# Four graph layers on one core: the first layer's sparse product in two float32r parts, its mask widened by GpSimd

## The chip, the core and the metric

The kernel runs on one core of a Trainium2 chip. The metric is the device time of one execution in microseconds; the median of three is compared. The engines are named as in the profile: PE is TensorE (PEld its weight loads), DVE VectorE, ACT ScalarE, POOL GpSimd, SP SyncE, which here issues most DMAs.

## The reference

Inputs are x (2708 rows of 128), adj (2708 x 2708, some 8 ones per row, each row divided by its count, so that it is a 0/1 mask times one value per row), and small weights. Four layers, each applied to a layer norm with relu and added to x:

```python
h = relu(layernorm(x));  x = x + L0(h, adj)     # hyperbolic: see below
h = relu(layernorm(x));  x = x + L1(h, adj)     # messages gelu(s_i + d_j + b), summed over edges, then an update
h = relu(layernorm(x));  x = x + relu(adj @ (h @ W2))
h = relu(layernorm(x));  x = x + h @ W_self + (adj @ h / deg) @ W_neigh

# L0, in short
h     = exp0(log0(x) @ embed);  h = h_add(h, embed_bias)
neigh = exp0(adj @ log0(h))                      # the sparse product of this case
out   = h_add(exp0(log0(concat(x, neigh)) @ layer), layer_bias)
```

exp0 and log0 scale a row by tanh(n)/n and arctanh(n)/n of its norm n.

## The kernel before

Rows are cut into T = 22 tiles of 128 (the last has 20 rows). Columns of the products go in blocks of four tiles, 512 columns, so there are 6 blocks; the last has 148 columns. `adj_t` is read in pieces of four row tiles by one block (`read_piece`), and each piece is turned into an fp8 0/1 `mask` by VectorE or ScalarE.

The sparse product of layer 0 is `yT = u^T mask`: for each block and each tile t, TensorE multiplies a 128x128 weight made of u's rows by `mask[:, t, block]` and adds into one PSUM bank. To keep float32 precision with an fp8 mask, `split` writes u as three bf16 parts that add up to it, and `add_product` issues one matmul for each part. `end_product` squares the sums into `hT`'s space and copies them to yT, from which `neighbours` takes norms, the product with `layer_w` and the row `own`. `update` then brings x forward for a list of blocks, normalises it, turns it with TensorE (`normal_tiles` into hT), multiplies by `msg_w` and writes d to two tables in HBM, `d_early` (first three blocks) and `d_hbm` (all).

Beside the product runs the search for the edges. `pack` sums the mask times powers of two, so that one word holds 22 tiles (the same mask columns as the product), `find_words` takes the 24 largest words of a row, `find_columns` and `lay_out` turn them into indices, and `pack_edges` into lists of edges. GpSimd's indirect DMAs then gather rows of d: 44 early ones (`gather_early`, from d_early), and in layer 1's loop 152 more (`messages`).

The code calls blocks in a hand-written order: product 0, 1 in two halves with the search for block 2 between, 2, neighbours of the first three, 3, three quarters of 4, update of the first three, first early gathers, the rest of 4, 5, then the search's remainder, pack_edges of the first three, neighbours and update of the last three. This is program order; a scheduler places the instructions within each engine's queue. After it, from layer 1's loop on, a planner with durations and due times writes the order, and `manual_schedule` keeps it.

SBUF space is handed out from pools on two sides. On the right side lie, before, `hT` (pool turned) and the low bf16 parts (pool parted); the same bf16 parts are used again in layers 1 and 2. The third layer widens its mask to float32r (`widen`, ScalarE) and uses two parts already.

Of the kernel before, what the change touches and what calls it, by code (L numbers as in the profile page):

```python
# [29 lines left out]
F32 = mybir.dt.float32  # L30
# [529 lines left out]
def sparse_stack(  # L560
# [37 lines left out]
    def cols(t0, t1):  # L598
        return slice(t0 * P, min(t1 * P, N))
# [12 lines left out]
    hT_held = ExitStack()  # L612
    hT = hT_held.enter_context(tc.tile_pool(name="turned", bufs=1, side="right")).tile(
        [P, NP], F32, name="hT"
    )
    tmp = upper.tile([P, T, D], F32, name="tmp")
    parted = min(16, T)
    parts_held = ExitStack()
    parts_low = parts_held.enter_context(tc.tile_pool(name="parted", bufs=1, side="right")).tile(
        [P, parted, 3, D], BF16, name="parts"  # L620
    )
    parts_high = state.tile([P, max(1, T - parted), 3, D], BF16, name="partsh")
# [123 lines left out]
    d_early = dram.tile([first_half * P + 1, D], F32, name="d_early")  # L746
    none = const.tile([1, D], F32, name="none")
    nc.gpsimd.memset(none, BIG)
    msg_w, msg_br, upd_w, upd_br, ln_wr, ln_br, w2_w, self_w, neigh_w = (
# [13 lines left out]

    def load_later():

        nc.gpsimd.dma_start(out=d_hbm[NP : NP + 1, :], in_=none)
        nc.gpsimd.dma_start(out=d_early[first_half * P :, :], in_=none)
        for w, src in (
            (msg_w, msg_wt),
            (upd_w, upd_wt),  # L770
            (w2_w, w2),
            (self_w, w_self),
            (neigh_w, w_neigh),
        ):
            nc.gpsimd.dma_start(out=w, in_=src.rearrange("(a p) o -> p a o", p=P))
        for r, src in ((msg_br, msg_b), (upd_br, upd_b), (ln_wr, ln_w), (ln_br, ln_b)):
            nc.gpsimd.dma_start(out=r, in_=src.partition_broadcast(P))
# [18 lines left out]

    def split(src, sl, left):

        nc.scalar.copy(part_of(sl, 0), src[:, sl, :])  # L799
        nc.vector.tensor_sub(left, src[:, sl, :], part_of(sl, 0))  # L800
        nc.scalar.copy(part_of(sl, 1), left)
        nc.vector.tensor_sub(part_of(sl, 2), left, part_of(sl, 1))  # L802


    unchecked = list(range(T))
# [5 lines left out]
    with ExitStack() as st:  # L811

        words_p = st.enter_context(tc.tile_pool(name="words", bufs=2))
        left_p = st.enter_context(tc.tile_pool(name="left", bufs=2))
        wide = st.enter_context(tc.tile_pool(name="wide0", bufs=1))
        small = st.enter_context(tc.tile_pool(name="small", bufs=1))
        pair_p = st.enter_context(tc.tile_pool(name="pair", bufs=2))
        ps_acc = st.enter_context(tc.tile_pool(name="ps_acc", bufs=2, space=PSUM))
# [7 lines left out]
        for t in range(T):  # L826
            nc.gpsimd.tensor_scalar_mul(shifts[:, t, :], ident, float(2 ** (T - 1 - t)))
# [4 lines left out]
        load_later()  # L832

# [135 lines left out]
        cand = spare[:, n_top : 4 * n_top].rearrange("p (t k s) -> p t k s", k=3, s=SLOTS)  # L969
        more = wide.tile([P, T], F32, name="more")  # L970

        def read_piece(b, g, vector=False, after=None):
# [231 lines left out]
        def pack_edges(b, after=None):  # L1204
# [5 lines left out]
            for k in range(n):  # L1210
                t = t0 + k
                before = pair_p.tile([P, EDGES], F16, tag="before", name=f"before{t}")
                with queue_behind(after):
# [12 lines left out]
                for q in range(NQ):  # L1226
# [6 lines left out]
                    )  # L1233
            ex = small.tile([P, BLOCK, NQ, TAIL + 3], F32, tag="ex", name=f"exs{b}")
            nc.scalar.copy(ex[:, :n], px[:, :, :, : TAIL + 3])
            m = n * NQ
            kth, past, jump = (
                small.tile([P, BLOCK * NQ], F32, tag=name, name=f"{name}{b}")[:, :m]
                for name in ("kth", "past", "jump")
            )  # L1240
            flat_ex = ex.rearrange("p t q c -> p (t q) c")[:, :m, :]
            edge = small.tile([P, BLOCK, NQ], F32, tag="edge", name=f"edge{b}")[:, :n, :]
            nc.vector.tensor_copy(edge, edge_p.unsqueeze(1).to_broadcast([P, n, NQ]))
# [11 lines left out]
            nc.vector.tensor_add(kth, kth, jump)  # L1255
            sel = small.tile([P, BLOCK * NQ, TAIL], F32, tag="sel", name=f"sel{b}")[:, :m, :]
            nc.vector.tensor_tensor(
# [5 lines left out]
            nc.vector.tensor_mul(sel, sel, flat_ex[:, :, :TAIL])  # L1263
            cf = small.tile([P, BLOCK * NQ], F32, tag="cf", name=f"cf{b}")[:, :m]
            nc.vector.tensor_reduce(cf, sel, AX.X, ALU.add)
# [7 lines left out]

        def begin_product(b):
            return ps_acc.tile([P, BANK], F32, tag="acc", name=f"acc{b}")

        def add_product(b, acc, ts, after=None):

            sl = cols(*blocks[b])
            w = sl.stop - sl.start  # L1280
            for t in ts:
                for k in range(3):
                    with queue_behind(after):
                        last = nc.tensor.matmul(  # L1284
                            acc[:, :w],
                            part_of(t, k),
                            mask[:, t, sl],
                            start=(t == 0 and k == 0),
                            stop=(t == T - 1 and k == 2),
                        )  # L1290
            return last

        def end_product(b, acc, sums):
# [4 lines left out]
            w = sl.stop - sl.start  # L1298
            sq = hT[:, t0 * P : t1 * P]
            if w < n * P:  # L1300
                nc.gpsimd.memset(sq[:, w : n * P], 0.0)
            nc.scalar.activation(sq[:, :w], acc[:, :w], AF.Square)
            nc.scalar.copy(yT[:, sl], acc[:, :w])
            ps, first = sums
            for k in range(n):
# [3 lines left out]
                )  # L1309

        def product(b, sums):
            acc = begin_product(b)
            add_product(b, acc, range(T))
            end_product(b, acc, sums)

        def neighbours(bs, sums):
# [21 lines left out]
            for b in bs:  # L1338
                g = groups[b]
                ps = tiles_times(g, yT, layer_w[:, 1, :], f"ne{b}")  # L1340
                for t in range(g.start, g.stop):
# [8 lines left out]
                    nc.scalar.activation(  # L1350
                        hT[:, t * P : (t + 1) * P],
                        own[:, t, :],
# [103 lines left out]
        nc.vector.tensor_mul(ca, ca, f)  # L1456
        scaled = nc.vector.tensor_mul(cb, cb, f)
        for g in pieces[:3] if nb > 1 else ():
            read_piece(1, g)
        for g, sl in enumerate(groups):  # L1460
            for t in range(sl.start, sl.stop):
# [12 lines left out]
        for g, sl in enumerate(groups):  # L1474
            nc.scalar.copy(own[:, sl, :], tiles_times(sl, hT, layer_w[:, 0, :], f"own{g}"))
        if NP > N:
# [20 lines left out]
        find_columns(groups[0])  # L1497
        product(0, sums)
        find_words(1, words_in(1), scaled)
        find_columns(groups[1])  # L1500
        acc = begin_product(1)
        add_product(1, acc, range(T // 2))
        find_words(2, words_in(2), scaled)
        find_columns(groups[2])
        read_block(3)
        add_product(1, acc, range(T // 2, T))
        end_product(1, acc, sums)
        lay_out(halves[0])
        find_words(3, words_in(3))
        read_block(4)  # L1510
        product(2, sums)
        neighbours([0, 1, 2], sums)
        read_block(5)
        sums = sums_of(late)
        product(3, sums)
# [24 lines left out]
        for b in late:  # L1540
            pack_edges(b)


# [1130 lines left out]
```

## Time and profile before

| | |
|---|---|
| measured runs | 549.23 us median (548.35 to 553.0) |
| profiled execution, its own time | 653.21 us |
| its span | 651.4 us |
| PE, DVE, ACT, POOL busy | 430.5, 412.4, 321.0, 224.0 us |
| granted TensorE clock, mean | 0.825 |
| DMA | 77.85 MB, mean 120 GB/s |

The profile is of one execution, which took longer than the measured runs. Busy time is summed over an engine's instructions; for TensorE the ends are modelled. A line like `L1284 PE MATMUL acc<-mask,parts` names the source line, the engine, the operation, and the output and inputs by tile. Line numbers in the prediction are those of the kernel before. The chain of waits goes back from the last instruction, at each step to what released it. "another core or an unknown queue" there means that no instruction in the trace accounts for the release.

### The profile page before, as it was taken

The numbers are of one execution on the slowest core, as the hardware profiler recorded it, in microseconds if no ns is written. First come the engines' busy times: TensorE is split into PE (matmuls) and PEld (weight loads), VectorE is DVE, ScalarE is ACT, GpSimd is POOL, SyncE is SP. The second block draws the span as 40 slices with busy tenths as digits, with TensorE's granted clock in tenths as the row PEclk, the third lists the DMA queues.
The fourth block names the chain that finished last, engine by engine and source line by source line (L and its number), as shares of the span: only waits on it lengthen the run. The fifth ranks groups of instructions, "written<-read, shape, count | busy, mean of one in ns | idle before, by whom it ended". The sixth has DMA issues, their size and how long they took to land.

```text
span 651.4 us, 8164 instructions
## 1 busy us (share of the span) xinstructions
PE 430.5 (66%) x2467; PEld 295.6 (45%) x2467; DVE 412.4 (63%) x1715; ACT 321.0 (49%) x634; POOL 224.0 (34%) x277
## 2 busy tenths in 40 slices
PE   2956999999930003632177777837577888899875
PEld 2642444756720002532064544534445544678764
DVE  6879596578832166642155654565567648799963
ACT  3788677714200122321043533746567662899821
POOL 8500000000477700277465655665676300000000
PEclk9987999799955555666558987967799889999979
DMA  8884798200321100121131112665475240017502
GB/s 282 265 288 151 260 351 284 79 2 10 110 52 50 48 1 12 37 52 52 34 88 41 41 41 78 225 204 192 148 254 167 94 165 7 2 37 291 198 18 74
DMA packets 39363, 77.85 MB, mean 120 GB/s; under 512 B 5231, under 2 KB 18151, under 8 KB 38267
## 3 DMA queue, kind: packets, MB, share of 16 engines
q1 hardware_dynamic: 30846, 63.15, 28.3%
q0 software_dynamic: 6720, 13.38, 8.0%
q10 hardware_dynamic: 1744, 0.72, 0.4%
q8 instruction: 21, 0.34, 0.2%
q14 instruction: 32, 0.25, 0.1%
HBM read 73.62 MB, written 3.62 MB: 119 GB/s over the span
## 4 chain that ended last, share of the span: by engine, by line
PE 37%; DVE 25%; another core or an unknown queue 14%; ACT 13%; issue 5%; DMA 3%; POOL 2%; ACTq 0%; DVEq 0%
PE acc L1284 10%; PE two L2113 7%; DVE eq L2486 4%; ACT eq L2154 3%; PE pk L1021 2%; PE msg L1876 2%; PE three L2300 2%; ACT wm L1709 2%; PE msg L1870 2%; DMA layer_w<-in_L_gnn_layer_dram 2%; PE d L941 1%; POOL g L1810 1%; PE u L1424 1%; PE nd L1333 1%
## 5 line engine op out<-in xcount | busy, mean ns | idle before, releaser
L1810 POOL DMA_INDIRECT g<-d_hbm,head_c x88 | 90.5, 1028 | 106.1 <-DVE v L1751 45.7
L2113 PE MATMUL two<-mask,parts 128*128 128x512 fp8e4 (+1 forms) x288 | 71.1, 385 | 12.7 <-ACT parts L2044 5.7
L1810 POOL DMA_INDIRECT gt<-d_hbm,tail_c x64 | 64.5, 1008 | 24.1 <-issue 18.7
L1487 POOL DMA_INDIRECT early<-d_early,early_c x44 | 44.6, 1013 | 73.1 <-DMA d_hbm<-v 60.0
L2300 PE MATMUL three<-wm,pair 128*128 128x512 f32 (+1 forms) x264 | 62.9, 388 | 1.9 <-ACT pair L2359 1.8
L1284 PE MATMUL acc<-mask,parts 128*128 128x512 fp8e4 (+1 forms) x288 | 59.6, 358 | 0.6 <-DVE parts L802 0.4
L1709 ACT CAST wm<-mask 128x2708 fp32r<-128x2708 fp8e4 x22 | 53.3, 2450 | 7.1 <-DVE u L2064 7.0
L2300 PEld LDWEIGHTS three<-wm,pair 128*128 128x128 f32 x264 | 47.4, 194 | 11.7 <-ACT pair L2359 2.3
L2113 PEld LDWEIGHTS <-parts 128*128 128x128 bf16 x288 | 29.0, 106 | 40.1 <-issue 13.2
L930 PE MATMUL hTpm<-ident,h 128*128 128x128 f32 x22 | 5.1, 350 | 61.0 <-ACT h L920 61.0
L1876 PE MATMUL msg<-rt,gt 128*128 128x128 f32 x128 | 22.4, 318 | 33.5 <-ACT gt L1925 32.3
L1284 PEld LDWEIGHTS <-parts 128*128 128x128 bf16 x288 | 26.7, 99 | 37.8 <-ACT parts L799 7.5
L992 ACT ACTIVATE mask<-a 128x2048 fp8e4<-128x2048 uint32 (+3 forms) x27 | 37.9, 1433 | 9.0 <-DMA a<-in_adj_t_dram 9.0
L1021 PE MATMUL pk<-mask,shifts 128*128 128x512 fp8e4 (+1 forms) x132 | 31.6, 377 | 12.0 <-ACT mask L992 12.0
L1876 PEld LDWEIGHTS msg<-rt,gt 128*128 128x128 f32 x128 | 19.1, 219 | 39.4 <-ACT gt L1925 36.5
L2154 ACT ACTIVATE eq<-eq 128x1354 fp8e4<-128x1354 fp8e4 x26 | 34.4, 1326 | 4.9 <-DVE eq L2148 3.2
L1870 PE MATMUL msg<-ident,g 128*128 128x128 f32 (+1 forms) x176 | 28.3, 311 | 11.8 <-ACT g L1918 9.9
L1886 PE MATMUL msg<-upd_w,aggs 128*128 128x128 f32 x44 | 13.3, 394 | 30.6 <-issue 15.9
L1870 PEld LDWEIGHTS msg<-ident,g 128*128 128x128 f32 (+1 forms) x176 | 25.4, 219 | 16.5 <-ACT g L1918 12.4
L1859 DVE TENSOR_TENSOR gt<-gt,msg 128x384 f32<-128x384 f32 (+1 forms) x22 | 11.9, 540 | 31.4 <-remote 18.6
L930 PEld LDWEIGHTS hTpm<-ident,h 128*128 128x128 f32 x22 | 3.5, 173 | 62.1 <-ACT h L920 61.9
L2486 DVE TENSOR_SCALAR_CACHE_REDUCE eq<-row,val 128x1354 fp8e4<-128x1354 f32 (+1 forms) x18 | 29.2, 1620 | 0.3
(457 smaller groups left out, 1024.7 us busy)
## 6 DMA issues: line engine op xcount, KB each, us to landing
a<-in_adj_t_dram SPq DMA_DIRECT2D x25, 1024.0 KB
hT<-in_adj_dram SPq DMA_DIRECT2D x26, 677.0 KB
row<-in_adj_dram SPq DMA_DIRECT2D x8, 1354.0 KB
a<-in_adj_t_dram SPq DMA_DIRECT2D x5, 296.0 KB
g<-d_hbm,head_c POOLq DMA_INDIRECT x88
a<-in_adj_t_dram SPq DMA_DIRECT2D x5, 256.0 KB
d_hbm<-v SPq DMA_DIRECT2D x5, 256.0 KB
out_dram<-x SPq DMA_DIRECT2D x5, 256.0 KB
```

The source lines that it names most:

```text
L992: nc.scalar.activation(mask[:, g : g + n, sl], bits[:, :n, :w], AF.Sign, saturate=False)
L1021: nc.tensor.matmul(pk[:, :w], shifts[:, t, :], mask[:, t, sl], start=(t == 0), stop=(t == T - 1))
L1284: last = nc.tensor.matmul(acc[:, :w], part_of(t, k), mask[:, t, sl], start=(t == 0 and k == 0), stop=(t == T - 1 and k == 2),)
L1487: nc.gpsimd.indirect_dma_start(out=early_d[t // EACH][:n, t % EACH, k, :], out_offset=None, in_=d_early, in_offset=bass.IndirectOffsetOnAx ...
L1709: nc.scalar.copy(m, mask[:, t, :])
L1810: nc.gpsimd.indirect_dma_start(out=g[:n, q, :], out_offset=None, in_=d_hbm, in_offset=bass.IndirectOffsetOnAxis(ap=table[:n, q : q + 1], a ...
L1870: nc.tensor.matmul(sums(), box["g"][:n, q, :], ident[:n, :], start=False, stop=False)
L1876: nc.tensor.matmul(sums(), box["gt"][:, q, :], box["rt"][:, q, :], start=False, stop=(q == nq - 1),)
L2113: nc.tensor.matmul(two[b][:, : sl.stop - sl.start], part_of(t, k), mask[:, t, sl], start=(t == 0 and k == 0), stop=(t == T - 1 and k == 2),)
L2154: nc.scalar.activation(eq[0][:n, : c1 - c0], eq[0][:n, : c1 - c0], AF.Copy, accum_out=same[:n, t, k : k + 1], saturate=False,)
L2300: nc.tensor.matmul(three[b][:, : sl.stop - sl.start], made["pair"][:, t, k, :], wide_mask[t][:, sl], start=(t == 0 and k == 0), stop=(t == ...
L2486: nc.vector.tensor_scalar(eq[:n, : c1 - c0], my["row"][:n, c0:c1], val[:n, t : t + 1], None, op0=ALU.is_equal, op1=ALU.add, accum_out=same ...
```

## The change

Layer 0's product uses two float32r parts of u: u itself as float32r, and the rest. They lie in six tiles, one per group (pool fresh). [...]the mask has to be widened: GpSimd copies it, piece by piece, into a ring of three buffers (pool pieces), two tiles by 512 columns, or one tile by the 660 columns of blocks 4 and 5 together. Those two blocks are multiplied in one pass, each weight serving both. `product` is a generator that yields after half of the tiles, where block 1 has the search for block 2 between.

To make room, the right side is used in two phases. First `hT` (pool rising), closed once `own` is computed, which now comes before the split; then fresh and pieces; and after the last product these are closed and `hT` (turned), the bf16 parts (parted) and a pool `edges` with the temporaries of `pack_edges` are laid over them. A tile of a new pool waits for the tiles whose space it takes. So `update` of the first three blocks and `pack_edges` come after the last product in the program. The squares go to the space of `tmp` (`sq_room`, `junk`). The row `none` (moved from the constants) and the turned weights `wT` now share the tag and the single buffer of `row_square`.

```diff
-    def split(src, sl, left):
-        nc.scalar.copy(part_of(sl, 0), src[:, sl, :])
-        nc.vector.tensor_sub(left, src[:, sl, :], part_of(sl, 0))
-        nc.scalar.copy(part_of(sl, 1), left)
-        nc.vector.tensor_sub(part_of(sl, 2), left, part_of(sl, 1))
...
+        none = small.tile([1, D], F32, tag="rsq", name="none")
+        nc.gpsimd.memset(none, BIG)
...
-            wT = pair_p.tile([P, P], F32, tag="wT", name=f"wT{name}")
+            wT = small.tile([P, P], F32, tag="rsq", name=f"wT{name}")
...
-                before = pair_p.tile([P, EDGES], F16, tag="before", name=f"before{t}")
+                before = edge_pool().tile([P, EDGES], F16, tag="before", name=f"before{t}", bufs=2)
...
-            for t in ts:
-                for k in range(3):
-                    with queue_behind(after):
-                        last = nc.tensor.matmul(
-                            acc[:, :w], part_of(t, k), mask[:, t, sl],
-                            start=(t == 0 and k == 0), stop=(t == T - 1 and k == 2),
-                        )
...
+        def pieces_of(bs):
+            sl = cols(blocks[bs[0]][0], blocks[bs[-1]][1])
+            n = 2 if len(bs) == 1 else 1
+            w = sl.stop - sl.start
+            for t in range(0, T, n):
+                m = later["ring"].tile([P, 2 * BANK], F32R, tag="piece", name=f"wide{bs[0]}_{t}")
+                m = m[:, : n * w].rearrange("p (n c) -> p n c", n=n)
+                nc.gpsimd.tensor_copy(m, mask[:, t : t + n, sl])
+                for k in range(n):
+                    yield t + k, m[:, k, :]
+
+        def product(bs, sums, some=None):
+            accs = some or [
+                ps_acc.tile([P, BANK], F32, tag="acc", name=f"acc{b}") for b in bs
+            ]
+            for t, m in pieces_of(bs):
+                for k in range(2):
+                    at = 0
+                    for b, acc in zip(bs, accs):
+                        sl = cols(*blocks[b])
+                        w = sl.stop - sl.start
+                        nc.tensor.matmul(
+                            acc[:, :w], two_of(t)[:, k, :], m[:, at : at + w],
+                            start=(t == 0 and k == 0), stop=(t == T - 1 and k == 1),
+                        )
+                        at += w
+                if t == T // 2 - 1:
+                    yield
+            for b, acc in zip(bs, accs):
+                end_product(b, acc, sums)
...
+        for g, sl in enumerate(groups):
+            nc.scalar.copy(own[:, sl, :], tiles_times(sl, hT, layer_w[:, 0, :], f"own{g}"))
+        hT_held.close()
...
-            left = left_p.tile([P, BLOCK, D], F32, tag="left", name=f"left{g}")
-            split(u, sl, left[:, : sl.stop - sl.start, :])
+            two = parts_of[g]
+            nc.scalar.copy(two[:, :, 0, :], u[:, sl, :])
+            nc.vector.tensor_sub(two[:, :, 1, :], u[:, sl, :], two[:, :, 0, :].bitcast(F32))
...
-        acc = begin_product(4)
-        split_at = 3 * T // 4
-        last = add_product(4, acc, range(split_at))
-        formed = update([0, 1, 2], nc.scalar.copy, last)
+        for _ in product([4, 5], sums):
+            pass
+        rising.close()
+        hT = hT_held.enter_context(
+            tc.tile_pool(name="turned", bufs=1, side="right", reuse_waits="tile")
+        ).tile([P, NP], F32, name="hT")
...
+        edges_held = ExitStack()
+        later["edges"] = edges_held.enter_context(
+            tc.tile_pool(name="edges", bufs=1, side="right", reuse_waits="tile")
+        )
+        formed = update([0, 1, 2], nc.scalar.copy, None)
         find_words(4, words[4], formed)
...
-        add_product(4, acc, range(split_at, T), latest["times"])
-        end_product(4, acc, sums)
         find_words(5, words[5], formed)
-        product(5, sums)
```

More of the change, by code (lines that the diff above doesn't have):

```diff
@@ L612, in sparse_stack @@
     hT_held = ExitStack()
-    hT = hT_held.enter_context(tc.tile_pool(name="turned", bufs=1, side="right")).tile(
-        [P, NP], F32, name="hT"
+    hT = hT_held.enter_context(tc.tile_pool(name="rising", bufs=1, side="right")).tile(
+        [P, NP], F32, name="hTr"
     )
@@ L618, in sparse_stack @@
     parts_held = ExitStack()
-    parts_low = parts_held.enter_context(tc.tile_pool(name="parted", bufs=1, side="right")).tile(
-        [P, parted, 3, D], BF16, name="parts"
-    )
     parts_high = state.tile([P, max(1, T - parted), 3, D], BF16, name="partsh")
@@ L746, in sparse_stack @@
     d_early = dram.tile([first_half * P + 1, D], F32, name="d_early")
-    none = const.tile([1, D], F32, name="none")
-    nc.gpsimd.memset(none, BIG)
     msg_w, msg_br, upd_w, upd_br, ln_wr, ln_br, w2_w, self_w, neigh_w = (
@@ L762, in sparse_stack, with load_later @@
     )
-    def load_later():
+    def load_later(none):
         nc.gpsimd.dma_start(out=d_hbm[NP : NP + 1, :], in_=none)
@@ L813, in sparse_stack @@
         words_p = st.enter_context(tc.tile_pool(name="words", bufs=2))
-        left_p = st.enter_context(tc.tile_pool(name="left", bufs=2))
         wide = st.enter_context(tc.tile_pool(name="wide0", bufs=1))
         small = st.enter_context(tc.tile_pool(name="small", bufs=1))
-        pair_p = st.enter_context(tc.tile_pool(name="pair", bufs=2))
         ps_acc = st.enter_context(tc.tile_pool(name="ps_acc", bufs=2, space=PSUM))
@@ L831, in sparse_stack @@
             nc.gpsimd.memset(share_of[:, k : k + 1], 1.0 / max(k, 1))
-        load_later()
+        load_later(none)
         names = {}
@@ L970, in sparse_stack @@
         more = wide.tile([P, T], F32, name="more")
+        sq_room = spare[:, 4 * n_top : 4 * n_top + BANK]
+        junk = spare[:, 4 * n_top + BANK : 4 * n_top + BANK + D]
         def read_piece(b, g, vector=False, after=None):
@@ L1233, in pack_edges @@
                     )
-            ex = small.tile([P, BLOCK, NQ, TAIL + 3], F32, tag="ex", name=f"exs{b}")
+            ex = edge_pool().tile([P, BLOCK, NQ, TAIL + 3], F32, tag="ex", name=f"exs{b}")
             nc.scalar.copy(ex[:, :n], px[:, :, :, : TAIL + 3])
@@ L1237, in pack_edges @@
             kth, past, jump = (
-                small.tile([P, BLOCK * NQ], F32, tag=name, name=f"{name}{b}")[:, :m]
+                edge_pool().tile([P, BLOCK * NQ], F32, tag=name, name=f"{name}{b}")[:, :m]
                 for name in ("kth", "past", "jump")
@@ L1241, in pack_edges @@
             flat_ex = ex.rearrange("p t q c -> p (t q) c")[:, :m, :]
-            edge = small.tile([P, BLOCK, NQ], F32, tag="edge", name=f"edge{b}")[:, :n, :]
+            edge = edge_pool().tile([P, BLOCK, NQ], F32, tag="edge", name=f"edge{b}")[:, :n, :]
             nc.vector.tensor_copy(edge, edge_p.unsqueeze(1).to_broadcast([P, n, NQ]))
@@ L1255, in pack_edges @@
             nc.vector.tensor_add(kth, kth, jump)
-            sel = small.tile([P, BLOCK * NQ, TAIL], F32, tag="sel", name=f"sel{b}")[:, :m, :]
+            sel = edge_pool().tile([P, BLOCK * NQ, TAIL], F32, tag="sel", name=f"sel{b}")[:, :m, :]
             nc.vector.tensor_tensor(
@@ L1263, in pack_edges @@
             nc.vector.tensor_mul(sel, sel, flat_ex[:, :, :TAIL])
-            cf = small.tile([P, BLOCK * NQ], F32, tag="cf", name=f"cf{b}")[:, :m]
+            cf = edge_pool().tile([P, BLOCK * NQ], F32, tag="cf", name=f"cf{b}")[:, :m]
             nc.vector.tensor_reduce(cf, sel, AX.X, ALU.add)
@@ L1272, in sums_of, with edge_pool @@
             return ps_one.tile([P, BANK], F32, tag="one", name=f"nsq{bs[0]}"), blocks[bs[0]][0]
[L1274 to L1279, printed above, removed]
-            w = sl.stop - sl.start
-            for t in ts:
-                for k in range(3):
-                    with queue_behind(after):
-                        last = nc.tensor.matmul(
+        later = {}
+        def edge_pool():
+            return later["edges"]
+        def pieces_of(bs):
+            sl = cols(blocks[bs[0]][0], blocks[bs[-1]][1])
+            n = 2 if len(bs) == 1 else 1
+            w = sl.stop - sl.start
+            for t in range(0, T, n):
[15 more added lines that the diff above has]
+                        nc.tensor.matmul(
                             acc[:, :w],
-                            part_of(t, k),
-                            mask[:, t, sl],
+                            two_of(t)[:, k, :],
+                            m[:, at : at + w],
                             start=(t == 0 and k == 0),
-                            stop=(t == T - 1 and k == 2),
+                            stop=(t == T - 1 and k == 1),
                         )
-            return last
+                        at += w
[3 more added lines that the diff above has]
+                end_product(b, acc, sums)
         def end_product(b, acc, sums):
@@ L1298, in end_product @@
             w = sl.stop - sl.start
-            sq = hT[:, t0 * P : t1 * P]
+            sq = sq_room[:, : n * P]
             if w < n * P:
-                nc.gpsimd.memset(sq[:, w : n * P], 0.0)
+                nc.gpsimd.memset(sq[:, w:], 0.0)
             nc.scalar.activation(sq[:, :w], acc[:, :w], AF.Square)
@@ L1309, in end_product @@
                 )
[L1311 to L1314, printed above, removed]
         def neighbours(bs, sums):
@@ L1350, in neighbours @@
                     nc.scalar.activation(
-                        hT[:, t * P : (t + 1) * P],
+                        junk,
                         own[:, t, :],
@@ L1457, in sparse_stack, with two_of @@
         scaled = nc.vector.tensor_mul(cb, cb, f)
+        for g, sl in enumerate(groups):
+            nc.scalar.copy(own[:, sl, :], tiles_times(sl, hT, layer_w[:, 0, :], f"own{g}"))
+        hT_held.close()
+        rising = ExitStack()
+        fresh = rising.enter_context(
+            tc.tile_pool(name="fresh", bufs=1, side="right", reuse_waits="tile")
+        )
+        parts_of = [
+            fresh.tile([P, sl.stop - sl.start, 2, D], F32R, name=f"fresh{g}")
+            for g, sl in enumerate(groups)
+        ]
+        later["ring"] = rising.enter_context(
+            tc.tile_pool(name="pieces", bufs=3, side="right", reuse_waits="tile")
+        )
+        def two_of(t):
+            return parts_of[t // BLOCK][:, t % BLOCK]
         for g in pieces[:3] if nb > 1 else ():
@@ L1473, in sparse_stack @@
             read_piece(2, g, k < 3, last if k < 3 else None)
-        for g, sl in enumerate(groups):
-            nc.scalar.copy(own[:, sl, :], tiles_times(sl, hT, layer_w[:, 0, :], f"own{g}"))
         if NP > N:
@@ L1497, in sparse_stack @@
         find_columns(groups[0])
-        product(0, sums)
+        for _ in product([0], sums):
+            pass
         find_words(1, words_in(1), scaled)
         find_columns(groups[1])
[L1501 to L1507, printed above, removed]
+        for _ in product([1], sums):
+            find_words(2, words_in(2), scaled)
+            find_columns(groups[2])
+            read_block(3)
         lay_out(halves[0])
@@ L1510, in sparse_stack @@
         read_block(4)
-        product(2, sums)
+        for _ in product([2], sums):
+            pass
         neighbours([0, 1, 2], sums)
@@ L1514, in sparse_stack @@
         sums = sums_of(late)
-        product(3, sums)
+        for _ in product([3], sums):
+            pass
         words = {b: words_in(b) for b in (4, 5)}
-        acc = begin_product(4)
-        split_at = 3 * T // 4
-        last = add_product(4, acc, range(split_at))
-        formed = update([0, 1, 2], nc.scalar.copy, last)
+        for _ in product([4, 5], sums):
+            pass
+        rising.close()
+        hT = hT_held.enter_context(
+            tc.tile_pool(name="turned", bufs=1, side="right", reuse_waits="tile")
+        ).tile([P, NP], F32, name="hT")
+        parts_low = parts_held.enter_context(
+            tc.tile_pool(name="parted", bufs=1, side="right", reuse_waits="tile")
+        ).tile([P, parted, 3, D], BF16, name="parts")
+        edges_held = ExitStack()
+        later["edges"] = edges_held.enter_context(
+            tc.tile_pool(name="edges", bufs=1, side="right", reuse_waits="tile")
+        )
+        formed = update([0, 1, 2], nc.scalar.copy, None)
         find_words(4, words[4], formed)
@@ L1541, in sparse_stack @@
             pack_edges(b)
+        edges_held.close()
     ps_acc = ctx.enter_context(tc.tile_pool(name="ps_sum", bufs=len(blocks), space=PSUM))
```

## Prediction

> **What bounds the kernel now.** I read the page's slices first, then a table by stretch of 20 us, the chain of waits in order of time, VectorE's waits between 57 and 173 us, and last the timelines at the joints. The table's columns are PE, PEld, DVE, ACT and POOL busy with their counts, PE clock, DMA share, GB/s:
>
> ```profile
> 60.00:80.00 20.00, 19.75 (x94) 8.71 (x93) 14.56 (x42) 14.21 (x28) 0.00 (x0) 1.00 0.80 273
> 80.00:100.00 20.00, 20.00 (x101) 9.76 (x99) 17.41 (x104) 15.68 (x15) 0.00 (x0) 1.00 0.97 337
> 100.00:120.00 20.00, 19.29 (x107) 11.14 (x106) 9.48 (x56) 13.96 (x15) 0.19 (x1) 0.98 0.75 241
> 120.00:140.00 20.00, 20.00 (x93) 11.67 (x92) 18.45 (x107) 8.41 (x35) 0.00 (x0) 0.85 0.04 10
> 140.00:160.00 20.00, 19.92 (x124) 11.07 (x123) 15.27 (x83) 7.92 (x19) 0.00 (x0) 1.00 0.01 1
> ```
>
> While the first layer's sparse product runs, TensorE is busy 99.0 of 100 us and GpSimd does nothing. TensorE is the bound there, and GpSimd is free to widen.
>
> ```profile
> 61.96 5.21 PE acc L1284 x23
> 177.90 13.19 another core or an unknown queue
> 213.20 10.93 another core or an unknown queue
> 225.28 7.95 another core or an unknown queue
> 636.72 2.30 PE three L2300 x10
> ```
>
> These lines of the chain of waits give two matmul prices: a bf16 part over 512 columns costs 5.21/23 = 0.226 us, a float32r part in the last layer, one weight load each, 0.23 us. They also show a stop that no engine explains. Such pieces are 14.5% of 651.4, some 94 us, all later than 177 us. The profiled execution took 653.2 us (span 651.4), 104 us over the median of 549.2; I take these stops for the profile's own and leave them out. Between 172.6 and 272.8 us they come to 41.4.
>
> ```profile
> 155.95 0.30 DVE L1214 TENSOR_SCALAR before<-edge_i,n_end 128x384 f16<-128x384 f16 x1
> 169.39 2.65 POOL L1487 DMA_INDIRECT early<-d_early,early_c  x1 [59.99 <-DMA d_hbm<-v]
> 272.81 1.17 POOL L1810 DMA_INDIRECT g<-d_hbm,head_c  x1 [45.73 <-DVE v L1751]
> ```
>
> The joints, from the timeline. The last product ends at E = 172.6. The 44 early gathers start at 169.4 and follow each other every 1.25 us (55 us). The main gathers, 152 of them, start at G = 272.8, or 231.4 without the stops, and from there GpSimd's queue paces the message loop. So this change is worth what it does to G. Two chains lead to G. GpSimd's own ends at 169.4 + 55 = 224.4, 7 us early. VectorE's ends last: from its first pack_edges instruction (155.95) through the late blocks' neighbours and update to G it needs 231.4 - 155.95 = 75.4 us.
>
> ```profile
> DVE wt L1050 <- ACT wt L1041: 11.9, 4, 6.6
> DVE n_nsq L1320 <- PE nsq L1307: 10.4, 1, 10.4
> DVE n_off L1189 <- PE po L1188: 1.6, 1, 1.6
> ```
>
> VectorE's waits from 57 to 173 us: nearly all its slack, 24 us, is waiting for TensorE's results.
>
> [...]The trace of before has no GpSimd copy. Its nearest row is the scaling of a 128x128 tile:
>
> ```profile
> L827 POOL TENSOR_SCALAR shifts<-ident 128x128 bf16<-128x128 f32 x22 | 11.5, 536 | 1.0
> ```
>
> These start every 0.565 us, so [...]at worst, 4.4 ns per element. [...]Before, they meet only at 4 to 17 us, during those scalings:
>
> ```profile
> 7.72 0.24 DVE L908 TENSOR_TENSOR n_tn<-n_tn 128x12 f32<-128x12 f32 x1
> 8.00 0.17 DVE L910 SCALAR_TENSOR_TENSOR n_an<-n_tn,n_an 128x12 f32<-128x12 f32 x1
> ```
>
> The first took 0.24 against 0.17 for the same line at 141.5 us, the second nothing more: if there is a lock, it is held for a small part of 0.565 us. That fits a short read of 128 elements, and doesn't decide what 1024 do.
>
> **The change part by part.**
>
> *Matmuls.* Removed: five blocks of 66 x 0.225 = 14.9 us and the last of 66 x 0.081 (ten took 0.81), together 79.6. Added: four blocks of 44 x 0.23 = 10.1, and for the last two together 44 x 0.30 = 13.2[...]; 53.7. TensorE gains 25.9. The first update's transposes and its products with msg_w (three times 1.6 us, now between product matmuls) move behind the products, 4.8 more. With nothing else in the way the products end at E' = 172.6 - 30.7 = 141.9.
>
> *Splitting.* One ScalarE copy (0.6 us) and one VectorE subtraction (0.6) go per group, 3.6 us each over six; the product could begin a little sooner.
>
> *Start.* The row none, the transposed weights and the row squares now share one buffer. In the changed order wTe waits for the two DMAs that read none; they are issued at 17.6 and 18.9 us and take over 1 us each to issue, so about 22 instead of 12.5, and the u products that need it begin some 10 us later; queued behind wTe on VectorE is a mask piece. But the relus and their statistics now run ahead of it, and so does the first logarithm, which today follows the last u. I cost this at 0, between -3 and +4.
>
> *Widening.* 44 pieces of 1024 elements and 22 of 660. Estimate[...]: 1.2 and 0.9 us, 72.6 us in all. TensorE uses up a piece in 4 x 0.23 = 0.92, so GpSimd now paces the products, three pieces ahead at most. From 57 us: product 0 ends near 68 (before 76), product 1 stands for the mask of block 2, complete at 80.8 today, product 2 for block 3's, 96.4; it ends at about 102 (before 116). The pieces earn 14 us by then. Product 3, with the neighbours' matmuls, to 120; packing 4 and 5 to 127; 19 pieces of 0.9 make E' = 145.
>
> *What moves behind E'.* pack_edges takes its tiles from space that the pieces leave, so its first instruction waits for TensorE and GpSimd, and behind it on VectorE stand find_columns, lay_out and the whole chain to G. Less the 1.6 us for po, G' = E' + 74. The transposes follow E' too: gathers start at about E' + 13, GpSimd's chain ends at E' + 68 and stays hidden. To break even, E' or VectorE's arrival at pack_edges, whichever is later, must be 157.4.
>
> [...]From 57 to 156 us VectorE runs 147 TENSOR_TENSOR and SCALAR_TENSOR_TENSOR with two SBUF inputs, 60 by 119 us and 87 after. [...]0.26 per instruction on average. So 60 cost 16 us, less the 6.6 it now waits at wt: product 2, through po, ends at 111. From there to pack_edges VectorE needs 36.5 today, 3.9 of it a wait; plus 87 x 0.26 = 22.6 makes 57 with its 2 of lead-in: 168. E' itself is about 157. G' = 168 + 74 = 242, 10.6 later than 231.4. Below: nothing (no lock). Above: in a chain of dependent instructions each can meet a new piece[...]; I halve that excess, and bound this case at +30. I take +11.
>
> **The sum.** +10.6 on 549.2: 560. Without the lock 145 + 74 - 231.4 = -12.4.
>
> **Rivals.**
> - *No lock to speak of* (the other side). For it: the chain at 7.5 to 10.3 us, hardly slowed. Against: [...]pieces eight times as long. It ends at 537. It decides from 0.13 us of wait per two-input instruction downward: VectorE has 157.4 - 138 = 19 us to lose over 147.
> - *A slow GpSimd.* [...]It decides from 1.68 us per large piece, where E' passes 157.4 unaided. At 4.4 ns (the scaling row taken as all per element) E' = 305 and 697. For it: that row.[...]
> - *The products gain nothing*: if mask pieces and lock eat just the 12 us, 549.
>
> **How the numbers follow.** Lock, pieces near 1.2 us: 0.42, 560, its own range 549 to 579. No lock: 0.26, 537. Slow GpSimd: 0.24. No effect: 0.08. The range 535 to 595 takes in the lock's and the start's bounds and the moderate slow case; what it leaves out is mostly the slow end. A measurement here tells about 1% from no change. Faster 0.27, same 0.11, slower 0.62.
>
> **What would show it.** In the profile after: pieces 1.2 us apart on POOL and TensorE idle before acc for GpSimd; two-input VectorE instructions of the neighbours' chain starting some 0.4 us apart, not 0.2; the first pack_edges instruction near 168, the main gathers 74 us later plus the profile's stops. It is wrong if that instruction starts before 157, if pieces stand over 1.7 us apart, or if the loop after G changes its length.

## The result, and the profile after

| | median, us | against the kernel before, same chip and time |
|---|---|---|
| before | 551.12 (548.35 to 553.52) | |
| after | 575.69 (574.38 to 576.57) | 1.0431, 95% interval 1.0389 to 1.0472 |

The change costs 24.6 us (4.3%) where 10.6 were forecast. The profiled execution of the changed kernel took 576.57 us, its span 574.8; its line numbers are its own. Unlike the profile of before it holds no stops that no engine accounts for.

The same stretches as before, in the same columns (PE, PEld, DVE, ACT and POOL busy with counts, PE clock, DMA share, GB/s):

```profile
60.00:80.00 20.00, 14.16 (x47) 8.28 (x47) 19.93 (x66) 14.36 (x32) 7.93 (x7) 0.79 0.47 157
80.00:100.00 20.00, 17.46 (x85) 12.31 (x85) 15.91 (x54) 9.75 (x11) 15.64 (x14) 1.00 0.78 277
100.00:120.00 20.00, 16.20 (x72) 11.04 (x72) 16.70 (x84) 11.60 (x11) 10.55 (x10) 0.91 0.81 280
120.00:140.00 20.00, 20.00 (x118) 17.09 (x117) 16.56 (x69) 12.92 (x19) 12.91 (x14) 1.00 0.50 152
140.00:160.00 20.00, 19.72 (x128) 15.25 (x126) 13.39 (x39) 11.02 (x35) 12.47 (x19) 1.00 0.19 51
```

TensorE's column has lost what it was full of: 87.5 us busy instead of 99.0. VectorE's has grown, 82.5 instead of 75.2, but with fewer instructions behind it: 312 in these 100 us instead of 392. An engine that is busier with fewer instructions has longer ones on average, and which ones is the first thing to look up.

The joints, from the timelines of the changed kernel:

```profile
180.39 0.30 DVE L1203 TENSOR_SCALAR before<-edge_i,n_end 128x384 f16<-128x384 f16 x1
193.61 1.36 POOL L1510 DMA_INDIRECT early<-d_early,early_c  x1 [14.83 <-DMA d_hbm<-v]
252.34 1.07 POOL L1841 DMA_INDIRECT g<-d_hbm,head_c  x1 [0.30 <-issue]
```

VectorE reaches pack_edges at 180.4 (before 155.95), the early gathers start at 193.6 (169.4), the main gathers at G = 252.3. For before, the prediction had to work out G from a profile with stops: 231.4. An experiment below that takes as long as the kernel before (b_hoist, 552.77 us) has a profile without them:

```profile
155.73 0.30 DVE L1214 TENSOR_SCALAR before<-edge_i,n_end 128x384 f16<-128x384 f16 x1
169.24 2.58 POOL L1492 DMA_INDIRECT early<-d_early,early_c  x1 [60.06 <-DMA d_hbm<-v]
229.04 1.14 POOL L1817 DMA_INDIRECT g<-d_hbm,head_c  x1 [1.38 <-issue]
```

The first two joints are those of before within 0.3 us; G is 229.0, and from here on that is before's G. So G is 23.3 us later in the changed kernel, and the two profiled executions (576.57 and 553.59 us) differ by 23.0: the whole loss lies ahead of the main gathers, and the loop behind them has kept its length.

Last, the widening: a group line (busy us, mean ns, then the idle time before them and what ended it), three stretches of GpSimd's queue, and TensorE's wait for pieces between 60 and 164 us (in all, times, longest):

```profile
L1276 POOL CAST wide<-mask 128x660 fp32r<-128x660 fp8e4 x22 | 15.4, 748 | 8.1 <-PE acc L1291 7.5 <-ACT mask L981 0.6
148.99 13.29 POOL L1276 CAST wide<-mask 128x660 fp32r<-128x660 fp8e4 x19 [7.53 <-PE acc L1291]
132.59 5.99 POOL L1276 CAST wide<-mask 128x1024 fp32r<-128x1024 fp8e4 x6 [0.71 <-PE acc L1291]
78.44 4.87 POOL L1276 CAST wide<-mask 128x1024 fp32r<-128x1024 fp8e4 x1 [2.02 <-PE acc L1291]
PE acc L1291 <- POOL wide L1276: 2.5, 1, 2.5
```

Back to back, a piece takes 5.99/6 = 1.00 us and 13.29/19 = 0.70. GpSimd is quick enough: it is busy 59.5 of the 100 us in the table above, and its waits are mostly for TensorE to give a piece back (7.5 of 8.1 us ahead of the 660-element copies). TensorE waits for a piece only once, 2.5 us. One copy, at 78.44, took 4.87 us; the last section comes back to it.

### The profile page after: what moved, and what is told of

Its sections match the earlier page's. It is cut to its first block, busy times and chain, and to the rows that moved or that the text cites. A ratio compares the mean times of both kernels' runs of the same rounds, so it can differ in the third digit from the quotient of the medians.

```text
span 574.8 us, 8047 instructions
## 1 busy us (share of the span) xinstructions
PE 412.0 (72%) x2335; PEld 305.0 (53%) x2335; DVE 437.3 (76%) x1709; ACT 317.8 (55%) x628; POOL 291.5 (51%) x343
## 4 chain that ended last, share of the span: by engine, by line
DVE 34%; PE 25%; POOL 13%; ACT 13%; issue 8%; DMA 6%; DVEq 0%; ACTq 0%; POOLq 0%
POOL g L1841 6%; PE two L2144 5%; DVE eq L2517 4%; POOL gt L1841 3%; PE acc L1291 3%; ACT wm L1740 2%; DMA g<-d_hbm,head_c 2%; PE three L2331 2%; ACT eq L2185 2%; POOL shifts L812 2%; PE pk L1010 2%; DVE r_all L1206 2%; PE msg L1907 2%; PE msg L1901 1%; DMA gt<-d_hbm,tail_c 1%
## 5 line engine op out<-in xcount | busy, mean ns | idle before, releaser
L1276 POOL CAST wide<-mask 128x1024 fp32r<-128x1024 fp8e4 (+1 forms) x66 | 64.7, 1017 | 69.6 <-PE acc L1291 68.1
L1841 POOL DMA_INDIRECT gt<-d_hbm,tail_c x64 | 66.8, 1044 | 19.5 <-issue 15.6
L2144 PE MATMUL two<-mask,parts 128*128 128x512 fp8e4 (+1 forms) x288 | 67.8, 373 | 6.6 <-ACT parts L2073 6.3
L1291 PE MATMUL acc<-wide,fresh 128*128 128x512 f32 (+1 forms) x264 | 65.4, 397 | 5.8 <-DVE fresh L1494 3.2
L1291 PEld LDWEIGHTS acc<-wide,fresh 128*128 128x128 f32 x264 | 47.1, 196 | 27.3 <-issue 10.2
L2144 PEld LDWEIGHTS <-parts 128*128 128x128 bf16 x288 | 28.1, 102 | 31.1 <-ACT parts L2073 7.5
L907 ACT ACTIVATE h<-x,n_nb,n_rstd 128x128 f32<-128x128 f32 x44 | 17.5, 483 | 32.3 <-DVE n_nb L901 32.3
L1907 PE MATMUL msg<-rt,gt 128*128 128x128 f32 x128 | 24.2, 336 | 10.0 <-ACT gt L1956 9.9
L1907 PEld LDWEIGHTS msg<-rt,gt 128*128 128x128 f32 x128 | 21.2, 237 | 17.1 <-ACT gt L1956 15.1
L2144 PE MATMUL two<-mask,partsh 128*128 128x512 fp8e4 (+1 forms) x108 | 25.1, 382 | 3.8 <-ACT partsh L2073 3.8
```

The costliest lines, as they stand in the source:

```text
L1276: nc.gpsimd.tensor_copy(m, mask[:, t : t + n, sl])
L1291: nc.tensor.matmul(acc[:, :w], two_of(t)[:, k, :], m[:, at : at + w], start=(t == 0 and k == 0), stop=(t == T - 1 and k == 1),)
L1841: nc.gpsimd.indirect_dma_start(out=g[:n, q, :], out_offset=None, in_=d_hbm, in_offset=bass.IndirectOffsetOnAxis(ap=table[:n, q : q + 1], a ...
L1907: nc.tensor.matmul(sums(), box["gt"][:, q, :], box["rt"][:, q, :], start=False, stop=(q == nq - 1),)
L2144: nc.tensor.matmul(two[b][:, : sl.stop - sl.start], part_of(t, k), mask[:, t, sl], start=(t == 0 and k == 0), stop=(t == T - 1 and k == 2),)
```

## Experiments

All differences are to the kernel before, run with them (551.1 to 552.9 us). G and "arrival" (VectorE's first pack_edges instruction) are from each kernel's timeline.

| kernel | time, us | difference | arrival | G |
|---|---|---|---|---|
| after | 575.69 | +24.6 | 180.4 | 252.3 |
| a_own: after, none in its own space | 569.18 | +16.8 | 174.3 | 244.7 |
| a_fill: after, fills for copies | 559.03 | +6.1 | 166.3 | 236.6 |
| a_own_fill: a_own and a_fill together | 550.46 | -2.4 | 155.1 | 225.4 |
| a_half: after, copies halved | 575.09 | +22.2 | 179.5 | 249.9 |
| b_share: before, shared buffer | 558.17 | +5.8 | 159.6 | 233.0 |
| b_copies: before, idle copies | 571.16 | +18.8 | 175.2 | 246.7 |
| b_order: before, products first | 559.20 | +6.9 | 155.5 | 237.4 |
| b_f16: before, two float16 parts | 549.04 | -3.9 | 150.1 | 225.1 |
| b_f16_order: b_f16 and b_order together | 548.48 | -3.3 | 150.2 | 222.9 |
| b_f16_hoist: b_f16, scalar part earlier | 540.24 | -11.5 | 141.8 | 217.2 |
| b_hoist: before, scalar part earlier | 552.77 | +1.0 | 155.7 | 229.0 |

In all of them the time goes with G, within 3 us. My theory after reading the trace: the loss is the shared buffer at the start, VectorE standing still while GpSimd copies, and the order behind the last product. The rival for each was that it is hidden.

**The start alone (b_share), and without it (a_own).**

```diff
# b_share
-    none = const.tile([1, D], F32, name="none")
+        none = small.tile([1, D], F32, tag="rsq", name="none")
-            wT = pair_p.tile([P, P], F32, tag="wT", name=f"wT{name}")
+            wT = small.tile([P, P], F32, tag="rsq", name=f"wT{name}")
# a_own
-        none = small.tile([1, D], F32, tag="rsq", name="none")
+        none = spare[:1, :D]
```

> The kernel before, with one part of the change alone: none, the transposed weights and the row squares share one buffer. Theory: +6 to +9 us on the kernel before (557-561 us), u products from some 29 us on and the v scaling at 60 instead of 52. Rival: the products of this kernel wait for TensorE anyway and take the delay up: 549-553 us.

> The changed kernel, with the row none back in space of its own (a slice of an array that is idle until 60 us), so that the transposed weights wTe no longer wait for the two DMAs that read it. Theory: those DMAs hold VectorE at wTe until 25.6 us and put own and the v scaling 8 us late; all that follows is a chain, so the time falls by 6 to 9 us, to 567-570 us, and the first u product starts near 15 us instead of 29.5. Rival: the start has cover (what I predicted: 0, between -3 and +4), so the time stays at 574-577 us although u starts earlier.

b_share is at 558.17, ratio 1.0128 (1.0096 to 1.0159); a_own at 569.18, 16.8 us over before, where the changed kernel is 24.6 over. The timelines of after and of a_own at the first transposed weight:

```profile
25.74 0.29 DVE L942 COPY wTe<-wte 128x128 f32<-128x128 f32 x1 [7.24 <-DMA d_early<-none]
12.50 0.27 DVE L942 COPY wTe<-wte 128x128 f32<-128x128 f32 x1
```

In the changed kernel VectorE stands 7.24 us at this copy for a DMA of one row. The v scaling starts at 60.05 there and at 51.80 in a_own. The start has no cover; it costs 5.8 us alone and 7.8 beside the rest, as my theory had it.

**The copies alone (b_copies).** A one-element copy (from gate) is to hold each burst back until its product begins, though some 660-element pieces of the last burst ran ahead, among the pieces of the one before; m lies in r_all, which is idle until pack_edges.

```diff
+                    if t == 0:
+                        gate = part_of(0, 0) if b == 0 else yT[:, cols(*blocks[b - 1])]
+                        nc.gpsimd.tensor_copy(m[:, :1], gate[:, :1])
+                    nc.gpsimd.tensor_copy(m, mask[:, t : t + n, cs])
```

> The kernel before, with 66 copies on GpSimd added that nobody reads: the same mask pieces to float32r (44 of 1024, 22 of 660 elements), written into an array that is idle until pack_edges, a burst of 11 (22 at last) as each product begins. TensorE's work, the order and the start are as before. Theory (VectorE's instructions stand still while a GpSimd piece runs): many VectorE instructions take 0.7 to 1.0 us instead of 0.17 to 0.25 during the bursts, some 20 us in all; VectorE's 24 us of waiting for TensorE take up part, so +4 to +15 us (555-566 us). Rival (no lock; VectorE's long instructions in the changed kernel come from something else): 549-553 us and instructions of the usual length.

+18.8 us (1.0376, 1.0308 to 1.0443), above what I had given it. Nobody reads these copies, TensorE's work is as before, and yet arrival is 19.5 us later. VectorE's timeline in b_copies, where a burst ends at 140, then the changed kernel's in the last product:

```profile
138.47 0.95 DVE L794 TENSOR_TENSOR n_qk<-n_qk,n_ak 128x12 f32<-128x12 f32 x1
139.45 0.65 DVE L795 SCALAR_TENSOR_TENSOR n_rk<-n_qk,n_rk 128x12 f32<-128x12 f32 x1
140.13 0.17 DVE L850 TENSOR_TENSOR n_nk<-n_ak,n_rk 128x12 f32<-128x12 f32 x1
148.96 0.17 DVE L787 SCALAR_TENSOR_TENSOR n_ru<-n_qu,n_ru 128x12 f32<-128x12 f32 x1
149.80 0.67 DVE L789 TENSOR_TENSOR n_qu<-n_qu,n_au 128x12 f32<-128x12 f32 x1
150.50 0.65 DVE L790 SCALAR_TENSOR_TENSOR n_ru<-n_qu,n_ru 128x12 f32<-128x12 f32 x1
```

Twelve elements per partition take 0.65 us beside a 660-element copy and 0.95 beside one of 1024, 0.17 when GpSimd doesn't copy. In the changed kernel they start 0.70 us apart, the spacing of the 660-element pieces: a chain of dependent instructions gets through one per piece. Set against the medians of like instructions before, VectorE's instructions between 60 and 173 us are 25 us too long in the changed kernel, and 23 in b_copies.

**Fills for copies (a_fill), and without the start (a_own_fill).**

```diff
-                nc.gpsimd.tensor_copy(m, mask[:, t : t + n, sl])
+                nc.gpsimd.memset(m.bitcast(F32), 1.0)
```

> The changed kernel, with each widening copy replaced by a fill of the same piece with ones (the mask does not enter the first layer's sum; all else is as it was): GpSimd writes as much and reads nothing. Theory (VectorE and GpSimd exclude each other over reads): VectorE's TENSOR_TENSOR and SCALAR_TENSOR_TENSOR go back to 0.17-0.25 us, the first pack_edges instruction comes 12 us or more before 180, and the time falls by 9 to 18 us, to 558-567 us. Rival (any GpSimd instruction holds VectorE, or VectorE only waits for late results): VectorE's long instructions stay and the time is 573-578 us.

> The changed kernel with fills instead of copies (the mask left out of the first layer's sum) and with none in space of its own: what is left of the change is fewer matmuls and the order. If order (+6.9 alone) and start (+5.8 alone) add up as in the runs so far, and fewer matmuls gain a few us, this is at 550-558 us. Rival: order and lock only cover each other, so that without the lock the order costs nothing and the matmuls' gain shows: 538-546 us.

a_fill is at 559.03 (1.0118, 1.0055 to 1.0181), a_own_fill at 550.46 (0.9964, 0.9938 to 0.9989). GpSimd writes as much (a 660-element fill every 0.66 us, 7.25/11) and reads nothing; of the changed kernel's +24.6 us, 6.1 are left. VectorE's timeline in a_fill while fills run:

```profile
129.29 0.89 DVE L781 TENSOR_SCALAR n_rl<-n_al 128x12 int32<-128x12 int32 x1
130.22 0.17 DVE L784 TENSOR_TENSOR n_ql<-n_rl 128x12 f32<-128x12 f32 x1
130.31 0.81 DVE L849 TENSOR_SCALAR n_s<-n_z 128x12 f32<-128x12 f32 x1
130.43 0.69 DVE L785 TENSOR_TENSOR n_ql<-n_ql,n_al 128x12 f32<-128x12 f32 x1
131.15 0.17 DVE L851 SCALAR_TENSOR_TENSOR n_s<-n_s,n_z 128x12 f32<-128x12 f32 x1
131.24 0.16 DVE L786 SCALAR_TENSOR_TENSOR n_ql<-n_ql 128x12 f32<-128x12 f32 x1
```

Instructions with two tensor inputs are back at 0.17, but for single ones like that at 130.43, which ends together with the held TENSOR_SCALAR ahead of it. Some TENSOR_SCALAR, with one input, still take up to 0.92 for 12 elements (at 128.34; 0.17 at 122.33, ahead of the fills), and a cast of 96 elements took 1.04 (at 69.45; 0.21 at 89.56). So two-input instructions were held beside copies and hardly beside fills, some TENSOR_SCALAR beside both (0.66 at 157.38 in the changed kernel). Why the two differ, no run shows. The fills are not free: by the count above, VectorE's instructions are still some 12 us too long in a_fill and 10 in a_own_fill, mostly TENSOR_SCALAR. Even so, with fills and without the start the changed kernel is a shade under the kernel before. That is where my sum put it (550-558), but not by that sum: b_f16_order below, with the same order and no work on GpSimd, doesn't pay for the order.

**Halved copies (a_half).**

```diff
-                nc.gpsimd.tensor_copy(m, mask[:, t : t + n, sl])
+                for half in (0, 1):
+                    part = (half, slice(0, w)) if n == 2 else (0, slice(half * c, half * c + c))
+                    nc.gpsimd.tensor_copy(m[:, part[0], part[1]], whole[:, part[0], part[1]])
```

> The changed kernel, each widening copy split in two instructions of half the size (512 and 330 elements), the same pieces of space, the same mask and sum. Theory (a VectorE instruction stands still until the GpSimd instruction under way has ended, and in a dependent chain each meets a new one): the long instructions shrink from 1.0 to some 0.55 us and from 0.65 to 0.4, VectorE's 25 us of standing still fall to 12-15 and the time to 564-570 us. Rival (what VectorE loses goes by GpSimd's busy time, not by the size of its instructions): 574-580 us, more if half pieces cost more than half.

575.09 us, no gain: half of my theory fell. The waits shrink, the time doesn't. The instruction at L790 that took 0.65 above:

```profile
149.91 0.38 DVE L790 SCALAR_TENSOR_TENSOR n_ru<-n_qu,n_ru 128x12 f32<-128x12 f32 x1
148.99 16.36 POOL L1279 CAST wide<-mask 128x330 fp32r<-128x330 fp8e4 x38 [6.61 <-PE acc L1294]
```

Each wait is as short as foretold, but a half piece takes 0.43 us (16.36/38), not 0.35, GpSimd copies for longer (75.8 us in all against 64.7) and catches more instructions: VectorE's excess is 22.5 us against 25. So what counts here seems to be how long GpSimd copies while VectorE has such instructions to issue, not how the copies are cut.

**The order alone (b_order).**

```diff
-        last = add_product(4, acc, range(split_at))
-        formed = update([0, 1, 2], nc.scalar.copy, last)
+        add_product(4, acc, range(T))
+        end_product(4, acc, sums)
+        product(5, sums)
+        formed = update([0, 1, 2], nc.scalar.copy, None)
```

> The kernel before, with one part of the change alone: products 4 and 5 are both complete before the first update's transposes and its products with msg_w. Theory: the early gathers start at 181-187 us instead of 169 and end at 236-242 us, behind the end of VectorE's own chain (231 us), so GpSimd's queue sets the start of the main gathers: +5 to +10 us (556-561 us). Rival (what I predicted for this step): the early gathers stay hidden behind VectorE's chain: 546-552 us.

+6.9 us (1.0142, 1.0072 to 1.0212). Arrival has not moved. From b_order's chain of waits, in order of time (start, length, engine, what):

```profile
236.19 0.89 POOL early L1487
237.39 0.95 POOL g L1808
```

The main gathers follow the last early one at once. GpSimd's chain, which starts with d_early, has become the last, and VectorE's v for layer 1, which starts at 226.93, waits for nobody.

**TensorE's gain alone (b_f16), with the order (b_f16_order), with ScalarE's queue cleared (b_f16_hoist), and that alone (b_hoist).**

```diff
# b_f16
-        nc.scalar.copy(part_of(sl, 1), left)
-        nc.vector.tensor_sub(part_of(sl, 2), left, part_of(sl, 1))
+        high, low = (part_of(sl, k).bitcast(F16) for k in range(2))
+        nc.scalar.copy(high, src[:, sl, :])
+        nc.vector.tensor_sub(low, src[:, sl, :], high)
...
-                for k in range(3):
+                for k in range(2):
# hoist: norm, log_factor and moebius leave update for weigh
         neighbours([0, 1, 2], sums)
+        weigh([0, 1, 2])
         read_block(5)
```

> The kernel before, with the first layer's sparse product in two float16 parts instead of three bf16 parts; the mask stays as it is and nothing is widened, order and start as before. TensorE's matmuls of this product fall from 396 to 264, 26.5 us. Theory (VectorE waits 24 us for TensorE there): VectorE reaches pack_edges some 10 us earlier and the time falls by 8 to 14 us, to 538-544 us. Rival (VectorE's own work and GpSimd's gathers set the end, so TensorE's gain is hidden): 549-553 us.

> The kernel before with two parts instead of three (float16, nothing widened) and with products 4 and 5 ahead of the first update's transposes: fewer matmuls and the order of the changed kernel, without GpSimd's copies and without the shared buffer. If the changed kernel is the sum of its four parts, this equals the changed kernel with fills and with none in its own space: 548-553 us. Rival (the float32 pieces themselves, their matmuls or their waits cost or gain something more): outside of 546-555 us.

> The kernel before with two float16 parts, and the scalar part of the first update (norm, logarithms, moebius) written ahead of block 5's mask pieces and of the words of blocks 4 and 5. Theory: with two parts VectorE's wait has only changed its partner, from TensorE to ScalarE, whose queue brings the second logarithm 7.0 us late behind those pieces; with that gone VectorE reaches pack_edges at 142-146 instead of 150 and the time falls by another 4 to 8 us, to 541-545 us. Rival (another wait takes its place, TensorE's or a mask piece's): 547-551 us.

> The kernel before, with three parts as it is, and the same scalar part of the first update written earlier. Theory: here TensorE is the late one (VectorE waits 10.4 us for its row sums), ScalarE's queue is not, so the time stays at 550-554 us. Rival (ScalarE's queue already costs something here): 545-549 us.

b_f16 is at 549.04 (0.9927, 0.9901 to 0.9953): of the 26.5 us that the 132 matmuls fewer are worth at the prediction's prices, 3.9 arrive. That is the rival's number, but not for the rival's reason. VectorE's waits in b_f16 from 57 to 173 us:

```profile
DVE n_f L865 <- ACT n_lm L859: 7.0, 1, 7.0
DVE wt L1049 <- ACT wt L1040: 6.9, 3, 3.7
DVE n_s L877 <- ACT n_e L876: 2.2, 1, 2.2
DVE n_au L847 <- ACT hT L1349: 2.1, 1, 2.1
DVE n_nsq L1319 <- PE nsq L1306: 1.0, 1, 1.0
```

Before, wt and n_nsq held 22.3 us; they now hold 7.9. But 11.3 us for ScalarE stand beside them that were 0.3. Its queue runs mask pieces, then the words' copies that wait for TensorE, then the logarithms. Written ahead of block 5's pieces, the logarithms come in time: the wait at n_f is gone, arrival is 141.8, and the time 540.24 us, 0.9789 of before (0.9764 to 0.9814), the fastest kernel of this study. With three parts the same edit is worth nothing (1.0011, 0.9990 to 1.0033), as TensorE is the late one there. b_f16_order, 548.48 (0.9943, 0.9922 to 0.9964), lies near a_own_fill's 550.46: with products that end at 138 us instead of b_order's 167 the order costs nothing more.

## Why the prediction was wrong

The direction and the mechanism that decides were right, the size was not: the gain of the matmuls was put 9 to 10 us too high, the start 6 to 8 us too low, and the lock some 4 us too high, which hid part of the other two. The parts, as forecast and as measured:

| part | forecast | measured |
|---|---|---|
| fewer matmuls, with the order | -12.4 | -2.4 to -3.3 (a_own_fill, b_f16_order) |
| shared buffer at the start | 0 | +5.8 (b_share), +7.8 and +8.5 (pairs with and without) |
| lock | +23 | +18.5 to +19.2 (the pairs), +18.8 (b_copies) |
| sum | +10.6 | +21 to +25 |

The lock's 23 is the step from the forecast without it (-12.4) to the one with it. A pair is two kernels that differ in this part alone: after and a_own, a_fill and a_own_fill for the start; after and a_fill, a_own and a_own_fill for the lock. As some TENSOR_SCALAR are still held beside fills (up to 0.92 us in a_fill), these last two pairs set copies against fills, not against nothing, and a_own_fill's -2.4 has that remainder in it; b_f16_order's -3.3 hasn't.

- *What bounds the kernel.* Right: the time is read from G. The stops of the profile of before were the profile's own: G is 229.0, 2.4 earlier than my 231.4. VectorE's 75.4 us from arrival to G is 73.3, and 70 to 75 in all kernels of the table but b_order (81.9), so whoever knows arrival knows G nearly. In after and the runs made from it this holds although GpSimd's chain ends last there: its early gathers hang on the same update of VectorE as arrival does.
- *Matmuls: the step that failed most.* "With nothing else in the way": there was something, ScalarE. I had read that VectorE's slack was waiting for TensorE and took all 12 us of gain at once, without asking which wait ends second. b_f16 moves arrival by 5.6 us, b_f16_hoist by 13.9, so the gain was there, but behind ScalarE's queue. TensorE's own part came as forecast: with the start undone the last product ends at 157.2 us (a_own; about 157 forecast), with fills at 145.2 (a_own_fill; 145 forecast without the lock). But blocks 4 and 5 did not share weight loads in the changed kernel: from 149 to 162 us its trace shows 78 loads beside 80 matmuls, and 660 columns took 0.35 us (15.02/43, from 148.31) where 0.30 were forecast. What failed is G' = E' + 74, with VectorE ready at 138 and waiting for E': it arrives at 155.1 in a_own_fill, 10 us after E', and at 150.2 in b_f16_order. Apart from what the fills hold, a_own_fill shows ScalarE again, at another place: VectorE stands 8.2 us for the squares of own, on ScalarE behind mask pieces and behind the squares of product 3, for which ScalarE itself waits (8.2 of the 19.4 us that VectorE waits from 52 to 181). That clearing ScalarE's queue would help the changed kernel itself was not tried.
- *Start: failed.* The wait at wTe was seen and timed almost right (22 forecast, 25.7 measured). What failed is "I cost this at 0": the relus and statistics that run ahead are not the late part. The logarithms and the scaling need the last u product, and every u product needs wTe.
- *Widening: right.* 1.00 and 0.70 us against 1.2 and 0.9 forecast, which were my estimate: the trace of before has no such copy. A line through the two measured times gives, as an estimate, 0.82 ns per element and 0.16 us fixed. The rival of a slow GpSimd falls.
- *The lock (VectorE's two-input instructions held beside GpSimd's copies): right in kind, near in size, wrong in how it comes about.* I spread 0.26 us over 147 two-input instructions; that size was my estimate, not shown by the trace of before. Measured are some 40 waits of 0.4 to 0.9 us each: a whole piece, since each instruction of a chain meets a new one; in my words the upper case. And some TENSOR_SCALAR and a cast, which I hadn't counted, are held too (0.66 us at 157.38 for 12 elements, 1.04 at 69.95 for 96). Fewer instructions, each for longer: 25 us in all, where 147 x 0.26 = 38 were forecast. That the time came out nearer (+19 against +23) is in part luck. Arrival, 168 forecast, was 174.3 with the start undone.
- *Behind E'.* The last product ends at 163.3 with the late start. "Stays hidden" was wrong for GpSimd's chain: its early gathers start 30 us after E', not 13, because VectorE's update ends only at 172.9, and G follows the last of them (251.15) at once. VectorE's v for layer 1 doesn't set G here: it starts at 253.13, after G. How much earlier G would come without GpSimd's chain was not tried. In before this chain had 1 us in reserve (b_hoist's last early gather starts at 226.77), not the 7 I had worked out as 44 x 1.25, and b_order pays for it. The profile of before had shown it, with its last early gather at 226.19:

```profile
226.19 0.90 POOL L1487 DMA_INDIRECT early<-d_early,early_c  x1 [0.31 <-issue]
```

- *pack_edges waiting for the pieces' space* never decides: VectorE comes 17 us after E' in the changed kernel and 10 in a_own_fill.

The rivals of no lock and of no effect fall with b_copies and a_fill. Not settled is how a_half's total stays so near the whole copies' when its stretches differ; that it follows from GpSimd's longer copying is argued from its busy time, not shown by a run of its own. Nor does any run take the fills' remaining hold away from the changed kernel.

## What to carry to other kernels

When a bound engine is relieved, don't credit the wait that goes: list who feeds the waiting engine next, by its queue, and credit only the distance to that one. Before work goes to an engine that looks idle, ask whom it may hold up: here 65 us of copies on an idle GpSimd held VectorE for 25 us and cost the kernel 19. And a shared buffer is a wait like any other. The saving of the matmuls itself was to be had from two float16 parts, with no copy at all.

## What the runs showed of the hardware

- A two-input VectorE instruction of 12 elements took mostly 0.65 us beside 660-element copies on GpSimd and 0.17 without (after, b_copies); beside 1024-element fills most took 0.17 and TENSOR_SCALAR up to 0.92 (a_fill).
- It goes the other way too: a 1024-element copy took 4.87 us at 78.44 us in the changed kernel and 5.6 at 73.53 in b_copies, instead of 1.0, while VectorE ran mask pieces (TENSOR_SCALAR, at their usual 1.22 us) and two-input subtractions one after another.
- MAX8 was not held: 0.49 us for two at 100.33 us in the changed kernel, during three copies from 99.89 to 103.16, as against 0.49 at 91.03 us in before, without copies.
- A float16 part as the weight with an fp8 operand was multiplied at the pace of a bf16 part: 6.27/29 = 0.216 us over 512 columns in b_f16's chain of waits; in before's chain 0.216 (9.93/46, at 148.50) to 0.226. The means of the largest group of these matmuls, whose ends are modelled, are 393 ns (x160) in b_f16 and, with three bf16 parts, 384 in b_hoist and 394 in b_order (x240 each).
